# A Fourier layer stack beside its read-out head: two chunks are paired, the accumulator banks become one tile, and some read-outs are cut in half

## The chip, the cores and the metric

One core of a Trainium2 chip runs the whole program once. The metric is the device time in microseconds (us) of that run, from its first to its last instruction. The parts of the core that matter here: TensorE (PE in the profile) multiplies matrices and leaves the results in PSUM, a memory of 8 banks with 512 float32 numbers in each of 128 partitions; ScalarE (ACT) and VectorE (DVE) read PSUM, apply a function or an addition, and write to the main on-chip memory. GpSimd (POOL) and SyncE (SP) only start transfers. Each engine works through its own instructions in the program's order, and waits at an instruction until what it needs has been done by the others.

## The reference

A batch of 8 images with 8 channels of 256 x 256 is normalised, goes through a Fourier neural operator in four groups, and then through a 3 x 3 maximum:

```python
h = _gconv1x1(h, fc0_w, fc0_b)
for i in range(4):
    h1 = _spectral_conv(h, sp_w1[i], sp_w2[i])    # rfft2, mix the 12 x 12 low modes, irfft2
    h2 = _gconv1x1(h, w_w[i], w_b[i])
    h = h1 + h2
    if i < 3:
        h = _gswish(h, betas[i])
h = _gswish(_gconv1x1(h, fc1_w, fc1_b), betas[3])  # 10 -> 128 channels in each group
return _gconv1x1(h, fc2_w, fc2_b)                  # 128 -> 2 channels in each group
...
x = x + _L0_conv_ref(_gn(x), ...)
x = x + _L1_conv_ref(_gn(x))                       # 3 x 3 dilation
```

All of it is float32. The kernel has the Fourier transforms as matrix products with small tables.

## The kernel before

While the four layers of image b are computed, the "head" (fc1, Silu, fc2) of image b - 1 is computed in between, step by step. A head has 128 steps. A step is one fc1 block; at every second step there is also an fc2 block, which sums two earlier steps.

PSUM is handed out in slots of two banks, four slots in all; a small result takes a slot too and uses one bank of it:

```python
def ps_z(name):
    return ps.tile([128, 2, 512], F32, tag="z", bufs=4, name=name)

def ps_a(name):
    return ps_z(name)[:, 0, :]
```

The head. `first(n)` is an fc1 block with its two Silu read-outs by ScalarE; `second(n)` is an fc2 block with its addition by VectorE:

```python
def first(n):
    ...
    pair = [ps_z(f"p_fc1_{b}_{n}_{i}") for i in range(2)]
    for g in range(G):
        mm(pair[g // 2][:, g % 2, :], w1[part(g), blk, :], hs[k][part(g), :], start=True, stop=True)
    for i in range(2):
        nc.scalar.activation(act[:, 2 * i : 2 * i + 2, :], pair[i], AF.Silu)

def second(n):
    ...
    y, acc = box["y"], ps_a(f"p_fc2_{b}_{n}")
    for i in range(2):
        act = acts.pop(n + i)
        for g in range(G):
            mm(acc[part(g), :], w2[:, g, 15 - rb - i : 47 - rb - i], act[:, g, :], start=i == 0, stop=i == 1)
    ...                                            # y = sums + y on VectorE

for n in range(STEPS):
    ...                                            # load of a later state
    if n % 2 == 0 and n > 3:
        second(n - 4)
    first(n)
    yield
second(STEPS - 4)
second(STEPS - 2)
```

A layer goes over 11 chunks of the image, two at a time. `burst(c)` is the inverse transform along a row (L490) added to the 1x1 convolution (L487, L484 in the first layer), read out by ScalarE with Silu. `turn(c)` transposes the chunk on VectorE, `transform(k)` is the forward transform along the columns (L455) of a pair of chunks, read out half by VectorE and half by ScalarE, and `gather(k)` (L469) sums its tiles:

```python
yield "even"                                       # brings the head to an even step
for k in range((NCH + 1) // 2):
    c = 2 * k
    burst(c)
    if k > 1:
        gather(k - 2)
    yield (1,)
    turn(c)
    if c + 1 < NCH:
        burst(c + 1)
    if k > 0:
        transform(k - 1)
    yield (1,)
    if c + 1 < NCH:
        turn(c + 1)
out_["sw"] = [load_sw(l + 1, 0), load_sw(l + 1, 1)]
gather(k - 1)
transform(k)
yield 2
gather(k)
yield 1
```

`yield (1,)` asks for exactly one head step at this place; these are the exact steps. `yield 2` and the like give a weight, and head steps are spread over such places by weight; these are the loose steps. They fall between the loops over chunks, where the low modes are mixed (VectorE) and the tables of the next layer are made. The fourth layer has its own loop, one burst and two exact steps at a time. The first image has no head beside it, and the head of the last image runs alone at the end.

The engines PE, DVE and ACT keep the order in which the program is written.

Of the kernel before, what the change touches and what calls it, by code (L numbers as in the profile page):

```python
# [10 lines left out]
F32 = mybir.dt.float32  # L11
I32 = mybir.dt.int32
AF = mybir.ActivationFunctionType
ALU = mybir.AluOpType
AX = mybir.AxisListType
PSUM = bass.MemoryType.PSUM
# [18 lines left out]
NCH = 11  # L35
# [4 lines left out]
STEPS = 128  # L40
# [5 lines left out]
def fno_dilate_kernel(ctx: ExitStack, tc: tile.TileContext, a: dict, out: bass.AP):  # L46
    nc = tc.nc
# [2 lines left out]

    const = ctx.enter_context(tc.tile_pool(name="const", bufs=1))
    sb = ctx.enter_context(tc.tile_pool(name="sb", bufs=2))
    ps = ctx.enter_context(tc.tile_pool(name="ps", bufs=2, space=PSUM))
    dram = ctx.enter_context(tc.tile_pool(name="dram", bufs=2, space=bass.MemoryType.DRAM))


    def ps_z(name):
        return ps.tile([128, 2, 512], F32, tag="z", bufs=4, name=name)

    def ps_a(name):  # L60
        return ps_z(name)[:, 0, :]
# [126 lines left out]


    alone = [True]  # L190

    def copy(i, dst, src):
        if alone[0] and i % 2:
            nc.scalar.activation(dst, src, AF.Identity)  # L194
        else:
            nc.vector.tensor_copy(dst, src)  # L196
# [234 lines left out]
    def layer(b, l, out_, stored, side):  # L431
        group_in_f = l % 2 == 1

        def turn(c):

            dst = turned[:, c % 3].rearrange("p (s f x) -> p f s x", s=2, f=NQ)
            for i in range(2):
                nc.vector.transpose(  # L438
                    dst[:, 2 * i : 2 * i + 2], h[:, c, 2 * i : 2 * i + 2].rearrange("p f (s x) -> p f s x", s=2))
# [37 lines left out]
        def burst(c):  # L477
            pair = [ps_z(f"p_z_{b}_{l}_{c}_{i}") for i in range(2)]
            for f in range(NQ):
                for q in range(NQ):  # L480
                    o = pair[q // 2][part(f), q % 2, :]
                    if l == 0:
                        k = slice(32 * q, 32 * q + 6)
                        mm(o, wcn[k, :], h[k, c, f, :], start=True, stop=False)  # L484
                    else:
                        g = f if group_in_f else q
                        mm(o, wt[part(q), l, g, :], h[part(q), c, f, :], start=True, stop=False)  # L487
            for s in range(2):
                for q in range(NQ):
                    mm(pair[q // 2][:, q % 2, HW * s : HW * (s + 1)],  # L490
                       zt[part(q), 2 * c + s].rearrange("p f o -> p (f o)"), binv[part(q), :],
                       start=False, stop=s == 1)
            for i in range(2):
                dst = h[:, c, 2 * i : 2 * i + 2, :]
                if l < 3:
                    nc.scalar.activation(dst, pair[i], AF.Silu)  # L496
                else:
                    nc.scalar.activation(dst, pair[i], AF.Identity, bias=bias3)  # L498
            if l == 3:
                nc.sync.dma_start(stored[c], h[:, c].rearrange("p f w -> p (f w)"))  # L500
# [20 lines left out]
            return  # L521
        yield "even"
        for k in range((NCH + 1) // 2):
            c = 2 * k
            burst(c)
            if k > 1:
                gather(k - 2)
            yield (1,)
            turn(c)
            if c + 1 < NCH:  # L530
                burst(c + 1)
            if k > 0:
                transform(k - 1)
            yield (1,)
            if c + 1 < NCH:
                turn(c + 1)
        out_["sw"] = [load_sw(l + 1, 0), load_sw(l + 1, 1)]
        gather(k - 1)
        transform(k)
# [74 lines left out]
    def head(b, stored, stats):  # L614
        hs, acts, box = {}, {}, {}
        last = b + 1 == n_img
        if last:
            for t in (ya[:, :, 0:1], ya[:, :, HW + 1 :], ya[:, 0, :], ya[:, 17, :]):
                nc.gpsimd.memset(t, -BIG)

        def load_state(k):

            if k < NQ * NCH:
                j, c = k // NCH, k % NCH
                hs[k] = sb.tile([128, PIX], F32, tag="hs", bufs=4, name=f"hs_{b}_{k}")
                nc.sync.dma_start(hs[k], stored[c][:, PIX * j : PIX * (j + 1)])

        def first(n):

            k, blk = n // 32 * NCH + n % 32 // NBLK, n % 32 % NBLK  # L630
            act = sb.tile([128, G, 512], F32, tag="act", bufs=4, name=f"act_{b}_{n}")
            pair = [ps_z(f"p_fc1_{b}_{n}_{i}") for i in range(2)]
            for g in range(G):
                mm(pair[g // 2][:, g % 2, :], w1[part(g), blk, :], hs[k][part(g), :], start=True, stop=True)  # L634
            for i in range(2):
                nc.scalar.activation(act[:, 2 * i : 2 * i + 2, :], pair[i], AF.Silu)  # L636
            acts[n] = act

        def second(n):

            t, rb = n // 16, n % 16
            if rb == 0:
                if last:
                    y = ya[:, 1 + 2 * t : 3 + 2 * t, 1 : HW + 1]
                else:
                    y = sb.tile([128, 512], F32, tag="yp", name=f"y_{b}_{t}")
                    y = y.rearrange("p (s w) -> p s w", s=2)
                box["y"] = y
                nc.sync.dma_start(
                    y, a["x"][b].rearrange("c (p t s w) -> (c p) t s w", p=16, t=8, s=2)[:, t])  # L650
            y, acc = box["y"], ps_a(f"p_fc2_{b}_{n}")
            sums = acc.rearrange("p (s w) -> p s w", s=2)
# [3 lines that stand above are left out]
                    mm(acc[part(g), :], w2[:, g, 15 - rb - i : 47 - rb - i], act[:, g, :],  # L656
                       start=i == 0, stop=i == 1)
            if rb == 0:
                nc.vector.scalar_tensor_tensor(y, sums, b2, y, ALU.add, ALU.add)  # L659
            else:  # L660
                nc.vector.tensor_tensor(y, sums, y, ALU.add)  # L661
            if rb == 14 and last:
                for i in range(2):
                    nc.vector.bn_stats(stats[:, 2 * t + i, :], y[:, i])  # L664
                dilate_early(t)
            elif rb == 14:
                nc.vector.bn_stats(stats[:, t, :], y.rearrange("p s w -> p (s w)"))
                whole = y_rows[b % 2][:]
                nc.gpsimd.dma_start(
                    bass.AP(whole.tensor, whole.offset + (1 + 2 * t) * HW, [[16 * HW, 128], [HW, 2], [1, HW]]), y)  # L670

        load_state(0)
        load_state(1)
        for n in range(STEPS):
            if n % 32 % NBLK == 0:
                load_state(n // 32 * NCH + n % 32 // NBLK + 2)
            if n % 2 == 0 and n > 3:
                second(n - 4)
            first(n)
            yield  # L680
        second(STEPS - 4)
        second(STEPS - 2)


# [53 lines left out]
    def tail():  # L738
        if tails and next(tails[0], tails) is tails:
            tails.pop(0)  # L740
# [3 lines left out]
    with tc.manual_schedule(engines={PE, DVE, ACT}):  # L744
        d = {}
        for _ in start(0, d):
            pass
        for b in range(n_img):
            stored = [dram.tile([128, NQ * PIX], F32, tag=f"hs{c}", name=f"stored_{b}_{c}") for c in range(NCH)]
            exact, loose, ahead = 0, 0, {}  # L750
            for n in layers(b, stored, d, start(b + 1, ahead)):
                if isinstance(n, str):
                    if count[0] % 2 != (n == "odd") and step():
                        share -= 1.0
                elif isinstance(n, tuple):
                    exact += sum(n)
                    for _ in range(sum(n)):
                        if scale and step():
                            tail()
                else:  # L760
                    loose += n
                    share += n * scale if scale else 0
                    while share >= 1.0:
                        share -= 1.0
                        step()
            scale = scale or (STEPS - exact) / loose
            d = ahead
            if b + 1 < n_img:
                stats_of[b] = sb.tile([128, 8, 6], F32, tag="bn_y", name=f"bn_y{b}")
            else:  # L770
                stats_of[b] = spare[:, 16384:16480].rearrange("p (n s) -> p n s", s=6)
            heads.append((b, head(b, stored, stats_of[b])))
            alone[0] = False
        while step():
            tail()
        for t in tails:
            for _ in t:
                pass
# [151 lines left out]
```

## Time and profile before

| | |
|---|---|
| device time, median of 3 | 4005.67 us (3990.84 to 4009.22) |
| span of the profiled run | 3994.4 us, granted TensorE clock 0.978 |
| PE busy | 3717.9 us (93%) |
| ACT busy | 2813.2 us (70%) |
| DVE busy | 2566.1 us (64%) |
| DMA | 86 GB/s on average |
| fc1 blocks (L634), PE busy | 1176.2 us |
| fc2 blocks (L656), PE busy | 994.1 us |
| Silu of fc1 (L636), ACT busy | 1960.7 us in 2048 instructions, mean 1026 ns |

A row of a profile table reads: line, engine, operation, what it writes and from what, shapes, count, then the busy time and the mean of one, and then the time that the engine was idle just before, with what ended it. In a timeline a row is a run of equal instructions: its start, its length, engine, line and count, and in brackets the idle time of the engine before it. "PEld" is the load of a matrix that stays in the array; it comes ahead of a matmul and may run beside an earlier one. One float32 matmul of the program is two rows (passes) of each in the trace.

### The profile page before, as it was taken

How to read it: one execution, taken by the hardware profiler on the slowest of the kernel's cores; microseconds unless marked ns; L12 is line 12 of the kernel's file. 1: busy time of each engine (PE TensorE's matmuls, PEld its weight loads, DVE VectorE, ACT ScalarE, POOL GpSimd, SP SyncE). 2: the span in 40 equal slices, each digit the busy share in tenths (PEclk: the TensorE clock that was granted, in tenths of full speed). 3: DMA queues.
4: the chain of work that ended last, by engine and by line, in shares of the span. 5: the costliest groups of instructions: out<-in, count | busy, mean ns of one | idle time of the engine just before them, and what ended most of it. 6: DMA issues, size and time to landing. Idle time of an engine off the chain costs nothing. (4 is left out here: it accounts for less than half of the span.)

```text
span 3994.4 us, 118622 instructions
## 1 busy us (share of the span) xinstructions
PE 3717.9 (93%) x53530; PEld 1443.4 (36%) x53530; DVE 2566.1 (64%) x3679; ACT 2813.2 (70%) x2945; POOL 117.0 (3%) x202
## 2 busy tenths in 40 slices
PE   5667999999999999999999999999999999999997
PEld 2334333433333333333333333333333333333221
DVE  6775665567676666766766676666776666673533
ACT  3335777777777777776777777777777777778886
POOL 1000000000000000000000000000000000000100
PEclk8878999999999999999999999999999999999998
DMA  3014111432125222251123511244121532115311
GB/s 86 15 37 169 52 38 41 148 113 67 59 73 175 77 57 68 79 192 53 58 60 104 185 51 49 59 145 139 57 62 49 181 92 67 59 51 196 100 48 47
DMA packets 113985, 345.05 MB, mean 86 GB/s; under 512 B 15768, under 2 KB 18392, under 8 KB 98056
## 3 DMA queue, kind: packets, MB, share of 16 engines
q1 hardware_dynamic: 95288, 276.33, 22.4%
q0 software_dynamic: 18192, 61.13, 4.6%
q8 instruction: 421, 6.90, 0.7%
q14 instruction: 84, 0.69, 0.1%
HBM read 213.40 MB, written 123.74 MB: 84 GB/s over the span
## 5 line engine op out<-in xcount | busy, mean ns | idle before, releaser
L636 ACT ACTIVATE act<-p_fc 128x1024 f32<-128x1024 f32 x2048 | 1960.7, 1026 | 751.2 <-PE p_fc L634 751.2
L634 PE MATMUL p_fc<-hs,c_w 32*128 32x512 f32 x8192 | 1176.2, 631 | 11.3 <-DVE turned L196 8.5
L656 PE MATMUL p_fc<-act,c_w 128*32 128x512 f32 x8192 | 994.1, 600 | 48.1 <-ACT act L636 37.2
L634 PEld LDWEIGHTS p_fc<-hs,c_w 32*128 32x128 f32 x8192 | 386.1, 183 | 687.8 <-ACT act L636 286.5
L438 DVE STREAM_TRANSPOSE turned<-h 128x1024 f32<-128x1024 f32 x528 | 622.7, 1218 | 15.0 <-ACT h L496 14.7
L496 ACT ACTIVATE h<-p_z 128x1024 f32<-128x1024 f32 x528 | 511.9, 1021 | 123.7 <-PE p_z L490 123.1
L661 DVE TENSOR_TENSOR y<-p_fc,y 128x512 f32<-128x512 f32 x392 | 269.9, 688 | 440.8 <-PE p_fc L656 439.0
L656 PEld LDWEIGHTS p_fc<-act,c_w 128*32 128x32 f32 x8192 | 234.9, 109 | 659.7 <-issue 390.9
L490 PE MATMUL p_z<-c_binv,zt 32*128 32x256 f32 x5632 | 410.2, 404 | 0.7 <-ACT zt L194 0.6
L490 PEld LDWEIGHTS p_z<-c_binv,zt 32*128 32x128 f32 x5632 | 259.1, 186 | 305.3 <-issue 294.6
L487 PE MATMUL p_z<-h,c_wt 32*32 32x512 f32 x8448 | 358.4, 601 | 11.5 <-DVE y L661 7.8
L455 PE MATMUL p_d<-turned,c_fw 32*32 32x480 f32 (+1 forms) x9216 | 305.8, 542 | 1.4 <-DVE turned L438 1.4
L196 DVE COPY zt<-p_g 128x264 f32<-128x264 f32 x300 | 162.6, 627 | 166.1 <-PE p_g L417 90.8
L202 DVE COPY turned<-p_d 128x960 f32<-128x960 f32 x144 | 154.5, 1073 | 165.2 <-PE p_d L455 165.2
L498 ACT ACTIVATE h<-p_z,c_bias 128x1024 f32<-128x1024 f32 x176 | 186.5, 1111 | 47.8 <-PE p_z L490 47.5
L370 DVE TENSOR_REDUCE S<-turned 128x80 f32<-128x800 f32 x192 | 188.7, 983 | 4.7
L367 DVE TENSOR_TENSOR turned<-t,B 128x800 f32<-128x800 f32 x192 | 188.4, 981 | 1.2 <-DMA t<-in_spw 1.1
L331 DVE STREAM_TRANSPOSE turned<-zt 128x960 f32<-128x960 f32 x96 | 175.5, 1854 | 0.8
L455 PEld LDWEIGHTS p_d<-turned,c_fw 32*32 32x32 f32 x9216 | 121.5, 103 | 142.3 <-issue 79.2
L200 ACT ACTIVATE turned<-p_d 128x960 f32<-128x960 f32 x144 | 130.2, 904 | 57.6 <-PE p_d L455 57.6
L487 PEld LDWEIGHTS p_z<-h,c_wt 32*32 32x32 f32 x8448 | 83.9, 103 | 238.5 <-issue 62.8
L469 PE MATMUL p_u<-turned,c_stack 128*32 128x480 f32 (+1 forms) x1152 | 136.5, 545 | 15.2 <-DVE turned L202 13.1
(171 smaller groups left out, 1934.1 us busy)
## 6 DMA issues: line engine op xcount, KB each, us to landing
stored<-h SPq DMA_DIRECT2D x88, 1024.0 KB
hs<-stored SPq DMA_DIRECT2D x352, 256.0 KB
t<-in_spw SPq DMA_DIRECT2D x96, 400.0 KB
yin<-y_rows POOLq DMA_DIRECT2D x56, 512.0 KB, 5.0
h<-in_xp SPq DMA_DIRECT2D x352, 48.0 KB
turned<-in_x SPq DMA_DIRECT2D x16, 1024.0 KB
y<-in_x SPq DMA_DIRECT2D x56, 256.0 KB
y_rows<-y POOLq DMA_DIRECT2D x56, 256.0 KB, 2.3
```

Of the source, the lines that this page charges most:

```text
L367: nc.vector.tensor_tensor(pr, sw[k], bt[:, k2, k].unsqueeze(2).to_broadcast([128, G, 2 * WID, WID]), ALU.mult)
L370: nc.vector.tensor_reduce(s[k2][:, k].rearrange("p g s o -> p (g s o)"), pr.rearrange("p g m i -> p (g m) i"), AX.X, ALU.add,)
L438: nc.vector.transpose(dst[:, 2 * i : 2 * i + 2], h[:, c, 2 * i : 2 * i + 2].rearrange("p f (s x) -> p f s x", s=2))
L455: mm(pair[q // 2][part(v % 4), q % 2, : 240 * n], fw8[part(q), v, :], t[part(q), :, :, v, : NBLK * WID], start=v < 4, stop=v >= 4)
L487: mm(o, wt[part(q), l, g, :], h[part(q), c, f, :], start=True, stop=False)
L490: mm(pair[q // 2][:, q % 2, HW * s : HW * (s + 1)], zt[part(q), 2 * c + s].rearrange("p f o -> p (f o)"), binv[part(q), :], start=False, s ...
L496: nc.scalar.activation(dst, pair[i], AF.Silu)
L498: nc.scalar.activation(dst, pair[i], AF.Identity, bias=bias3)
L634: mm(pair[g // 2][:, g % 2, :], w1[part(g), blk, :], hs[k][part(g), :], start=True, stop=True)
L636: nc.scalar.activation(act[:, 2 * i : 2 * i + 2, :], pair[i], AF.Silu)
L656: mm(acc[part(g), :], w2[:, g, 15 - rb - i : 47 - rb - i], act[:, g, :], start=i == 0, stop=i == 1)
L661: nc.vector.tensor_tensor(y, sums, y, ALU.add)
```

## The change

It does four things.

1. All of PSUM is one tile of 8 banks, and the slots are cut out of it in turn. What waits for a bank is then found bank by bank, and no longer slot by slot.
2. In the first three layers, the two bursts of a pair come one after the other, then the gather, then two head steps, then the transform. The aim is that TensorE changes less often between matmul shapes.
3. The fc2 block comes at the end of each odd step and not at the start of each even one, so that two exact steps are fc1, fc1, fc2.
4. In even loose steps, the first of the two Silu read-outs is cut into its two banks, so that its first bank comes free earlier; the fc2 block that follows uses that bank.

```diff
-    ps = ctx.enter_context(tc.tile_pool(name="ps", bufs=2, space=PSUM))
+    ps = ctx.enter_context(tc.tile_pool(name="ps", bufs=1, space=PSUM))
...
+    banks = ps.tile([128, 8, 512], F32, tag="z", name="banks")
+    ring = [0]
     def ps_z(name):
-        return ps.tile([128, 2, 512], F32, tag="z", bufs=4, name=name)
+        i = ring[0]
+        ring[0] = (i + 2) % 8
+        return banks[:, i : i + 2, :]
...
+    exact_step = [False]
...
         for k in range((NCH + 1) // 2):
-            c = 2 * k
-            burst(c)
+            for c in range(2 * k, min(2 * k + 2, NCH)):
+                burst(c)
             if k > 1:
                 gather(k - 2)
+            turn(2 * k)
             yield (1,)
-            turn(c)
-            if c + 1 < NCH:
-                burst(c + 1)
+            yield (1,)
             if k > 0:
                 transform(k - 1)
-            yield (1,)
-            if c + 1 < NCH:
-                turn(c + 1)
+            if 2 * k + 1 < NCH:
+                turn(2 * k + 1)
...
-            for i in range(2):
-                nc.scalar.activation(act[:, 2 * i : 2 * i + 2, :], pair[i], AF.Silu)
+            if n % 2 == 0 and not exact_step[0]:
+                nc.scalar.activation(act[:, 0, :], pair[0][:, 0], AF.Silu)
+                nc.scalar.activation(act[:, 1, :], pair[0][:, 1], AF.Silu)
+            else:
+                nc.scalar.activation(act[:, 0:2, :], pair[0], AF.Silu)
+            nc.scalar.activation(act[:, 2:4, :], pair[1], AF.Silu)
...
-            if n % 2 == 0 and n > 3:
-                second(n - 4)
             first(n)
+            if n % 2 and n > 2:
+                second(n - 3)
             yield
-        second(STEPS - 4)
         second(STEPS - 2)
...
                     exact += sum(n)
+                    exact_step[0] = True
                     for _ in range(sum(n)):
                         if scale and step():
                             tail()
+                    exact_step[0] = False
```

## The prediction

> **What bounds the kernel now.** I read the busy times and slices of the page first, then the list of waits, then timelines of three stretches.
>
> ```profile
> PE 3717.9 (93%) x53530; PEld 1443.4 (36%) x53530; DVE 2566.1 (64%) x3679; ACT 2813.2 (70%) x2945; POOL 117.0 (3%) x202
> ...
> L636 ACT ACTIVATE act<-p_fc 128x1024 f32<-128x1024 f32 x2048 | 1960.7, 1026 | 751.2 <-PE p_fc L634 751.2
> ```
>
> TensorE sets the time: 93% busy, and ScalarE waits 751 us for it. In the list of waits its own weight loads still wait for ScalarE:
>
> ```profile
> PEld p_fc L634 <- ACT act L636: 286.5, 404, 0.8
> ...
> PEld p_fc L656 <- ACT act L636: 197.4, 230, 1.4
> ```
>
> A late weight load is not lost time while an earlier matmul still runs, so the worth of these waits has to be read from starts of blocks. First a loose stretch in which only fc1, fc1, fc2 follow each other:
>
> ```profile
> 1529.32 0.16 PEld L656 LDWEIGHTS p_fc<-act,c_w 128*32 128x32 f32 x8 [1.11 <-ACT act L636]
> ...
> 1531.18 0.31 PEld L634 LDWEIGHTS p_fc<-hs,c_w 32*128 32x128 f32 x8 [0.84 <-ACT act L636]
> ...
> 1532.41 3.77 ACT L636 ACTIVATE act<-p_fc 128x1024 f32<-128x1024 f32 x4 [0.40 <-PE p_fc L634]
> 1533.49 0.16 PEld L656 LDWEIGHTS p_fc<-act,c_w 128*32 128x32 f32 x8 [1.07 <-ACT act L636]
> ```
>
> fc2 to fc2 is 4.17 us. fc2 takes 1.86 of it (1529.32 to 1531.18); from the first fc1 to the next fc2 it is 2.31. The read-outs start 1.23 us after the first fc1 does, the first of them is done some 1.02 later, at 1533.43, and fc2 starts at 1533.49: it waits for the bank of exactly that read-out.
>
> Next one full pair of chunks in the layer loop:
>
> ```profile
> 1483.87 1.14 PE L634 MATMUL p_fc<-hs,c_w 32*128 32x512 f32 x8
> ...
> 1485.00 1.33 PE L487 MATMUL p_z<-h,c_wt 32*32 32x512 f32 x32
> ...
> 1486.26 1.15 PE L490 MATMUL p_z<-c_binv,zt 32*128 32x256 f32 x16
> ...
> 1487.33 1.01 PE L469 MATMUL p_u<-turned,c_stack 128*32 128x480 f32 x8
> ...
> 1488.16 1.90 PE L656 MATMUL p_fc<-act,c_w 128*32 128x512 f32 x16
> ...
> 1489.99 1.14 PE L634 MATMUL p_fc<-hs,c_w 32*128 32x512 f32 x8
> 1491.06 1.18 PE L487 MATMUL p_z<-h,c_wt 32*32 32x512 f32 x32
> ...
> 1492.18 1.15 PE L490 MATMUL p_z<-c_binv,zt 32*128 32x256 f32 x16
> ...
> 1493.25 2.24 PE L455 MATMUL p_d<-turned,c_fw 32*32 32x480 f32 x64
> ...
> 1495.43 1.14 PE L634 MATMUL p_fc<-hs,c_w 32*128 32x512 f32 x8
> ```
>
> One pair is 11.56 us, with hardly an idle moment. The shape behind PE changes eight times (only L469 to L656 keep theirs). Where the shape changes, an fc1 block is 1.07 us (1489.99 to 1491.06); where two fc1 follow each other without a stall, the second starts 0.88 after the first (1521.93 to 1522.81). The step between two waves of passes is 0.43, so two passes are 0.86 and a change costs about 0.21, half before and half after. The z block at 1485.00 is 0.14 longer than that at 1491.06; it waits for the transform's banks.
>
> **What the Trainium skill says.** "TensorEngine Tiling (Array Packing)", Key Properties: changing the tiling mode, not just the tile, drains the TensorEngine. The trace agrees, at about 0.21 us a change. "ScalarE: Activation LUTs", What ACT_TABLE_LOAD costs: an ACTIVATE takes 186 ns plus 0.833 ns an element, and back-to-back ones overlap by about 93. For 1024 elements that is 1.04 us; the trace has 1.026, and four in a row in 3.77, so 0.92 each. "PSUM — Partial Sum Buffer", PSUM bank collisions raise a hardware error: guard PSUM by bank and quadrant. So a slot whose first bank was read alone can be given back by halves, which is what the single tile allows; the program's list of waits shows that fc2 of a loose step then waits for the first half alone.
>
> **Part 1: the halved read-out.** From the rows above, a half is 1.03 - 0.43 = 0.60 us when it starts alone and 0.92 - 0.43 = 0.49 behind another (estimates from the trace). Then fc2's bank is free at 1.23 + 0.60 + 0.05 = 1.88 after the first fc1, and fc2 could start at 0.88 + 1.07 = 1.95, not at 2.31. That 0.36 isn't all kept. fc1 of the next pair then starts at 1.95 + 1.85 = 3.80, but its second slot is that of the third full read-out: 1.23 + 0.60 + 0.49 + 2 x 0.92 = 4.16. Followed through two pairs, with ScalarE now at 2 x 0.49 + 3 x 0.92 = 3.74 a pair: pair one is 4.15 and pair two 3.80, so 3.97 on average, 0.19 below 4.16. The built program before has 155 runs of fc1, fc1, fc2, of which 64 are in the last head alone: 155 x 0.19 = 29 us, and some 3 for pairs that get into this form. **-32 us.** There are 512 even steps, of which 29 in each of seven heads are exact, so 309 are halved; the extra instruction costs 309 x 0.07 = 22 us on ScalarE, beside TensorE.
>
> **Part 2: full pairs.** New order: z, L490, z, L490, L469, fc1, fc1, fc2, L455, and L455 to z keeps its shape. Seven changes: 11.56 less 0.21, less the 0.2 of stalls now, is 11.15 without stalls. New stalls, from z at 0: L490 starts at 0.97 and 3.11, gather at 4.19, fc1 at 5.16. Read-outs start 1.19 after L490: those of the first burst end at 3.18 and 4.10, those of the second (from 4.30) at 5.32 and 6.24. The first fc1 needs three of the four slots' history: its second half waits for 5.37 (+0.2), the second fc1 for 6.29 (hidden by that), fc2 for the full read-out that runs 6.40 to 7.42 (+0.17; exact steps are not halved). L455 starts at 9.32, the next z at 11.38. **-0.17 a pair**, for k = 2 to 4.
>
> **Part 3: the ends of the loop.** At k = 0 there is neither gather nor transform. Now it takes 1453.40 to 1461.96, 8.56 us. In the new order the second fc1's halves wait for the second burst's read-outs (5.47 and 6.39), fc2 starts at 7.36 and the next z at 9.21: **+0.65**. At k = 1, 11.27 for 11.48: **-0.2**. At k = 5 the fc1 between transform and gather is gone:
>
> ```profile
> 1514.18 2.24 PE L455 MATMUL p_d<-turned,c_fw 32*32 32x480 f32 x64
> ...
> 1516.35 0.31 PEld L634 LDWEIGHTS p_fc<-hs,c_w 32*128 32x128 f32 x8 [0.79 <-ACT act L636]
> ...
> 1517.73 0.19 PEld L469 LDWEIGHTS p_u<-turned,c_stack 128*32 128x32 f32 x8 [1.07 <-ACT turned L200]
> ...
> 1518.70 0.99 PEld L455 LDWEIGHTS p_d<-turned,c_fw 32*32 32x32 f32 x64 [0.79 <-issue]
> ```
>
> The gather needs the transform's read-outs, which end 3.5 us after its start; fc1 fills that now. Image 0, which has no head, shows the bubble bare: its transform to gather takes 3.92 us and not 2.17. Other stalls of this pair get shorter; counted through it is 11.6 for 10.59, **+1.1**. One layer: 0.65 - 0.2 - 3 x 0.17 + 1.1 = +1.05, and 3 layers x 7 images give **+22 us**.
>
> **Part 4: the entry.** In the first and third layer the loop is now entered behind fc1, fc1, and z then waits for both read-outs of the first (1576.72, with most of its passes only at 1577.64). Behind fc2 most of it falls away: 0.9 x 14 = **-12 us**. Image 0: 0.2 x 12 = **-2**. The fourth layer keeps its order on TensorE: 0.
>
> Sum: -32 + 22 - 12 - 2 = -24, so 4005.7 - 24 = **3982 us**.
>
> **The rivals.** (a) All stalls vanish: 155 x 0.36 = 56, 126 pairs x 0.21 = 26, the 12 of the entry and no bubble: about 3910. For it: PE is the bound. Against it: four slots, and two bursts that leave ScalarE four read-outs deep (3.77 us) when fc1 comes. (b) ScalarE takes over: with 76% load inside a pair, any delay of its queue meets PE several times. If each of 126 pairs had 0.5 us more stall than I count, 4045. For it: fc1, fc2 and L455 each start within 0.2 us of a read-out's end in my sums. Against it: PE's stalls overlap and don't add up. (c) It is a wash: savings in loose steps and bubbles at k = 0 and 5 cancel, 4000. My sum is between (a) and (c). That VectorE becomes the bound I hold unlikely: 48.1 us busy in the 66.7 of a layer loop (1453.40 to 1520.10, windows view).
>
> **Range and chances.** Part 1 may be 15 to 50, Part 2 and 3 together 0 to 45, the runs before spread by 18. So 3940 to 4020. Faster by over 2% is below 3926 and needs most of (a): 0.08. Slower by over 2% is above 4086: 0.03. Within: 0.89.
>
> **What would show it.** Right: fc2 to fc2 about 3.97 in loose runs; 11.4 from pair to pair; 9.2 at k = 0; some 1.4 us of PE idle ahead of the last gathers; about 309 more Silu instructions, the 512-element ones near 0.6 us; PE busy near 3700. Wrong: pairs below 11.2 or above 11.8, loose runs still at 4.16, or a longer fourth layer, which I left out.

## The result and the profile after

The kernel after takes 4052.61 us (median of 4 runs, 4044.92 to 4054.53), the kernel before 4001.77 us on the same chip. The ratio is 1.0126, 95% interval 1.0097 to 1.0154: slower by 1.3%. The prediction was 3982 us in a range of 3940 to 4020.

The lines are numbered anew in the kernel after: fc1 is L638, fc2 L665, and its y-addition L670 (L668 for the first of a sum). Of fc1's Silu read-outs, L641 and L642 are the two halves, L644 is a full first one and L645 the second. z is L493, the inverse transform L496, the column transform L461, the gather L475. The page of the kernel after, first its busy times, then its costliest Silu row:

```profile
PE 3753.9 (93%) x53530; PEld 1508.2 (37%) x53530; DVE 2557.3 (63%) x3679; ACT 2816.7 (70%) x3254; POOL 117.0 (3%) x202
...
L645 ACT ACTIVATE act<-banks 128x1024 f32<-128x1024 f32 x1024 | 1063.0, 1038 | 1.7 <-PE banks L638 1.7
```

The 309 extra read-outs are there (3254 for 2945), and the busy shares are those of before within a point. TensorE's busy time is 36 us up, where the prediction had it near 3700; nothing on the page names the loss. Two lines of the list of waits (total, times, longest):

```profile
PEld banks L638 <- ACT act L645: 176.8, 257, 0.9
...
PEld banks L665 <- ACT act L641: 106.2, 140, 0.8
```

fc1's waits for its Silu are shorter: 232 us with those for L644 (55.3), where they were 286.5. fc2's are longer: 312 us with the other three Silu lines (100.5, 62.7, 42.5), where they were 197.4. As a late load need not cost time, the starts of blocks say more. A loose stretch with fc1, fc1, fc2 alone, from the timeline of the weight loads:

```profile
1557.53 0.16 PEld L665 LDWEIGHTS banks<-act,c_w 128*32 128x32 f32 x8 [0.76 <-ACT act L642]
...
1559.38 0.31 PEld L638 LDWEIGHTS banks<-hs,c_w 32*128 32x128 f32 x8 [0.84 <-ACT act L644]
...
1561.44 0.16 PEld L665 LDWEIGHTS banks<-act,c_w 128*32 128x32 f32 x8 [0.76 <-ACT act L641]
```

fc2 to fc2 is 3.91 us here (1557.53 to 1561.44), where it was 4.17. Over all such runs of the two traces (155 before, 162 after) the mean falls from 4.24 to 4.11 us. So the halves do their work, by 0.13 us a run. One pair of the layer loop, TensorE alone:

```profile
1511.93 2.19 PE L461 MATMUL banks<-turned,c_fw 32*32 32x480 f32 x61
1513.57 0.59 PE L493 MATMUL banks<-h,c_wt 32*32 32x512 f32 x1
...
1515.16 1.15 PE L496 MATMUL banks<-c_binv,zt 32*128 32x256 f32 x16
...
1518.43 1.01 PE L475 MATMUL banks<-turned,c_stack 128*32 128x480 f32 x8
1519.37 2.29 PE L638 MATMUL banks<-hs,c_w 32*128 32x512 f32 x16
1521.68 1.92 PE L665 MATMUL banks<-act,c_w 128*32 128x512 f32 x16
1523.53 1.02 PE L461 MATMUL banks<-turned,c_fw 32*32 32x480 f32 x22
```

From L461 to L461 it is 11.60 us, before 11.56 (the last row ends with the window). And the end of the loop, where the transform of the last full pair is followed at once by its gather:

```profile
1544.55 2.24 PE L461 MATMUL banks<-turned,c_fw 32*32 32x480 f32 x64
1548.19 1.01 PE L475 MATMUL banks<-turned,c_stack 128*32 128x480 f32 x8 [1.40 <-DVE turned L208]
```

TensorE stands empty for 1.40 us ahead of L475.

To see where the time arises, the table adds up the stretches between the starts of TensorE's blocks over the seven images that have a head beside them. A loop goes from its first burst to the first block behind its last transform. The two profiled runs are 58 us apart:

| us | before | after | fc2 moved alone | pair loop alone | one tile, halves |
|---|---|---|---|---|---|
| stretches between the loops | 1326 | 1357 | 1379 | 1328 | 1316 |
| loops of layers 1 to 3 | 1437 | 1472 | 1468 | 1568 | 1445 |
| loop of the fourth layer | 548 | 543 | 534 | 550 | 556 |
| last head alone | 298 | 293 | 302 | 298 | 294 |

Between before and after, the stretches lose 31 and the loops 35; the fourth layer and the last head win 5 each. The three columns on the right are experiments told below.

### The profile page after: what moved, and what is told of

Same layout as the page of the kernel before. It is cut to its first block, busy times and chain, and to the rows that moved or that the text cites. A ratio compares the mean times of both kernels' runs of the same rounds, so it can differ in the third digit from the quotient of the medians.

```text
span 4052.7 us, 119481 instructions
## 1 busy us (share of the span) xinstructions
PE 3753.9 (93%) x53530; PEld 1508.2 (37%) x53530; DVE 2557.3 (63%) x3679; ACT 2816.7 (70%) x3254; POOL 117.0 (3%) x202
## 5 line engine op out<-in xcount | busy, mean ns | idle before, releaser
L638 PE MATMUL banks<-hs,c_w 32*128 32x512 f32 x8192 | 1252.8, 635 | 28.4 <-DVE turned L202 8.4
L645 ACT ACTIVATE act<-banks 128x1024 f32<-128x1024 f32 x1024 | 1063.0, 1038 | 1.7 <-PE banks L638 1.7
L665 PE MATMUL banks<-act,c_w 128*32 128x512 f32 x8192 | 997.7, 605 | 11.6 <-ACT h L504 9.5
L644 ACT ACTIVATE act<-banks 128x1024 f32<-128x1024 f32 x715 | 739.5, 1034 | 182.4 <-PE banks L638 162.5
L638 PEld LDWEIGHTS banks<-hs,c_w 32*128 32x128 f32 x8192 | 444.3, 184 | 647.5 <-ACT act L645 176.8
L502 ACT ACTIVATE h<-banks 128x1024 f32<-128x1024 f32 x528 | 511.7, 1021 | 222.0 <-PE banks L496 220.3
L670 DVE TENSOR_TENSOR y<-banks,y 128x512 f32<-128x512 f32 x392 | 270.2, 689 | 566.1 <-PE banks L665 318.3
L665 PEld LDWEIGHTS banks<-act,c_w 128*32 128x32 f32 x8192 | 215.5, 110 | 722.3 <-issue 343.1
L641 ACT ACTIVATE act<-banks 128x512 f32<-128x512 f32 x309 | 184.5, 597 | 345.1 <-PE banks L638 340.9
L496 PE MATMUL banks<-c_binv,zt 32*128 32x256 f32 x5632 | 408.4, 403 | 0.2 <-issue 0.2
L496 PEld LDWEIGHTS banks<-c_binv,zt 32*128 32x128 f32 x5632 | 258.2, 185 | 304.6 <-issue 295.7
L493 PE MATMUL banks<-h,c_wt 32*32 32x512 f32 x8448 | 350.3, 601 | 1.1 <-DVE y L668 0.8
L461 PE MATMUL banks<-turned,c_fw 32*32 32x480 f32 (+1 forms) x9216 | 305.5, 538 | 3.0 <-DVE turned L444 3.0
L461 PEld LDWEIGHTS banks<-turned,c_fw 32*32 32x32 f32 x9216 | 120.0, 103 | 193.3 <-issue 87.8
L642 ACT ACTIVATE act<-banks 128x512 f32<-128x512 f32 x309 | 183.1, 592 | 0.0
```

The source lines that it names most:

```text
L461: mm(pair[q // 2][part(v % 4), q % 2, : 240 * n], fw8[part(q), v, :], t[part(q), :, :, v, : NBLK * WID], start=v < 4, stop=v >= 4)
L496: mm(pair[q // 2][:, q % 2, HW * s : HW * (s + 1)], zt[part(q), 2 * c + s].rearrange("p f o -> p (f o)"), binv[part(q), :], start=False, s ...
L644: nc.scalar.activation(act[:, 0:2, :], pair[0], AF.Silu)
L645: nc.scalar.activation(act[:, 2:4, :], pair[1], AF.Silu)
```

## The experiments

**One number needed to read them.** The granted clock of TensorE differs from kernel to kernel (means from 0.969 to 0.978), and at half clock TensorE's work takes about twice as long (in b_halves the fc2 block at 3250.62 us, with 2.3 us of it at half clock, takes 3.04 us for the usual 1.92). Over 46 runs of the kernel before, the span multiplied by its own granted clock scatters by 2.3 us (standard deviation), the span itself by 5.5. I call this product the full-clock time: it shows what the order of the program costs, apart from the clock. It is worked out from the means of all runs of a kernel.

| kernel | time, us | ratio to before | mean clock | full-clock time, us |
|---|---|---|---|---|
| before | 4000 | 1 | 0.977 | 3905 |
| after | 4052.6 | 1.0126 (1.0097 to 1.0154) | 0.976 | 3952 |
| b_tile | 4014.9 | 1.0046 (1.0032 to 1.0060) | 0.976 | 3916 |
| b_halves | 4005.3 | 1.0020 (1.0010 to 1.0030) | 0.972 | 3893 |
| b_fc2end | 4068.2 | 1.0184 (1.0170 to 1.0198) | 0.977 | 3974 |
| b_pairs | 4133.4 | 1.0347 (1.0333 to 1.0361) | 0.971 | 4013 |
| a_fc2start | 4129.8 | 1.0329 (1.0313 to 1.0344) | 0.969 | 3996 |
| a_last | 4034.8 | 1.0094 (1.0079 to 1.0109) | 0.973 | 3924 |
| a_full | 4073.8 | 1.0195 (1.0173 to 1.0217) | 0.977 | 3976 |
| a_loose | 4025.4 | 1.0074 (1.0059 to 1.0089) | 0.972 | 3910 |
| a_fix | 3995.5 | 0.9987 (0.9979 to 0.9996) | 0.972 | 3881 |
| b_rows | 4006.3 | 1.0013 (1.0005 to 1.0021) | 0.978 | 3915 |
| b_fourth | 3997.7 | 0.9986 (0.9973 to 0.9999) | 0.973 | 3886 |
| a_noadd | 3995.2 | 0.9989 (0.9978 to 1.0000) | 0.976 | 3898 |
| a_loose_noadd | 3998.0 | 0.9997 (0.9989 to 1.0005) | 0.971 | 3880 |
| b_rows_late | 3987.6 | 0.9967 (0.9953 to 0.9981) | 0.978 | 3896 |
| a_fix_rows | 3976.2 | 0.9936 (0.9919 to 0.9953) | 0.978 | 3885 |

Names with b_ start from the kernel before, with a_ from the kernel after. My theory, V below, was formed from the trace of after: fc2's new place spoils the order of VectorE's work between the loops, and both ends of the loop lose time.

### The parts one by one, added to the kernel before

**b_tile**, one tile alone:

```diff
-        return ps.tile([128, 2, 512], F32, tag="z", bufs=4, name=name)
+        return banks[:, i : i + 2, :]          # ring of 8 banks in one tile
```

> The kernel before with PSUM as one tile and nothing else. Theory V (the stretches outside the loops lose their time because fc2 at the end of the odd step puts its y-addition at a later place in VectorE's queue; the loops lose theirs at both ends): within 5 us of the kernel before, about 4002, since the waits found in the trace of after are all on the readers of the very bank that is written. Rival T (one tile for all of PSUM adds waits that separate buffers don't have): 4020 to 4035, with the loss spread over the loops and the stretches alike.

Measured 4014.9: between the theories, a loss of 0.46%, of which 11 us are left at full clock (3916 for 3905). Its trace is 22 us longer than that of before: 11 of them lie in the loops of layers 1 to 3 and the rest is spread. So the tile isn't free, as I had thought, but it isn't the main loss either. What the tile's cost consists of was not followed up.

**b_halves**, the halved read-outs on top of it:

```diff
+            if n % 2 == 0 and not exact_step[0]:
+                nc.scalar.activation(act[:, 0, :], pair[0][:, 0], AF.Silu)
+                nc.scalar.activation(act[:, 1, :], pair[0][:, 1], AF.Silu)
+            else:
+                nc.scalar.activation(act[:, 0:2, :], pair[0], AF.Silu)
```

> The kernel before with one tile and the even step's first read-out halved outside the loops. Theory V: 3980 to 4003, because halving frees a bank some 0.45 us earlier and harms nothing by itself. Rival H (309 more Silu instructions at about 0.2 us of fixed cost each lengthen ScalarE's queue, and that is the loss outside the loops): 4025 to 4035, all of it outside the loops.

Measured 4005.3, 10 us less than with the tile alone and 23 less at full clock (3893 for 3916). The stretches between the loops fall by 10 against before. Rival H is out; theory V's range is missed by 2 us. The halves gain, and more than half of it goes to a lower clock, 0.972 for 0.976.

**b_fc2end**, fc2 at the end of the odd step, four separate slots as before:

```diff
-            if n % 2 == 0 and n > 3:
-                second(n - 4)
             first(n)
+            if n % 2 and n > 2:
+                second(n - 3)
```

> The kernel before with fc2 at the end of the odd step instead of the start of the even one, nothing else. Theory V: the stretches outside the loops get about 30 us longer (as in the kernel after), so 4025 to 4040, with TensorE idle ahead of the matmuls of the mixing, and VectorE idle ahead of its y-additions longer than before. Rivals T and H: no loss from this part, 3995 to 4005.

Measured 4068.2: 72 us lost, more than theory V said. By the table, 53 lie between the loops and 31 in them; the fourth layer wins 14. This part alone is slower than the whole change. The fc2 block itself has moved ahead in the program's order: it now stands before whatever the layer has between two steps, and no longer behind it. The y-additions show it; first before, then this kernel, each from the list of VectorE's waits (total, times, longest):

```profile
DVE y L661 <- PE p_fc L656: 439.0, 310, 6.5
```

```profile
DVE y L661 <- PE p_fc L656: 663.9, 352, 5.7
```

VectorE stands 225 us longer ahead of the same additions, with whatever is queued behind them. (Ahead of the first addition of each sum, L659, it stands 24 us less.) In the stretches between the loops alone, its idle time ahead of all y-additions is 271 us, before 150.

**b_pairs**, the pair loop alone (the loop as in the diff of the change):

```diff
-            burst(c)
+            for c in range(2 * k, min(2 * k + 2, NCH)):
+                burst(c)
...
+            yield (1,)
             yield (1,)
             if k > 0:
                 transform(k - 1)
```

> The kernel before with the loop in pairs (two bursts, turn, two head steps, transform), nothing else. Theory V: the loops lose what they lose in the kernel after, some 35 us from the first and the last turn of the loop (about 30 from the empty TensorE ahead of the last gathers), the stretches outside nothing: 4030 to 4045. Rivals T and H: the same loss in the loops, so this run tells only whether the losses of the parts add up; if it is near 4002, the loss at the ends of the loop needs fc2's new place as well.

Measured 4133.4. The stretches lose nothing, as theory V said, but the loops lose 131 us and not 35. Some 26 of these are half clock in the first layer's loops. By the starts of the blocks a pair takes 12.41 us (second layer of image 3), and the transform starts 2.15 us after the second fc1, where 1.07 is free of waits. The second fc1 stops halfway:

```profile
1546.24 0.30 PEld L632 LDWEIGHTS p_fc<-hs,c_w 32*128 32x128 f32 x4 [0.89 <-DVE y L659]
```

Its second slot is the one that fc2, two blocks ahead of it, took, and the y-addition that reads that fc2 (1545.53 to 1546.18) stands on VectorE behind two transposes. In the kernel after, fc2 comes behind the two fc1, and they don't need its slot. The losses of the parts don't add up; each of the two orders mends part of what the other breaks.

### One part undone in the kernel after

**a_fc2start**, fc2 back at the start of the even step everywhere:

```diff
+            if n % 2 == 0 and n > 3:
+                second(n - 4)
             first(n)
-            if n % 2 and n > 2:
-                second(n - 3)
```

> The kernel after with fc2 back at the start of the even step: the pair loop, the one tile and the halved read-outs stay. Theory V: outside the loops it returns to the kernel before with halves (about 40 us less than after over the seven images), inside the loops it costs what the pair loop alone cost (+137 on before), so 4125 to 4145. Rival (the losses of the pair loop came from its being tried with full read-outs and four buffers, and one tile mends them): 4015 to 4060.

Measured 4129.8: the pair loop needs fc2 at the end of the step, with or without the tile. The stretches fall to 1315 us, level with b_halves.

**a_last**, for the last single chunk one head step on each side of the transform:

```diff
             yield (1,)
-            yield (1,)
+            if 2 * k + 1 < NCH:
+                yield (1,)
             if k > 0:
                 transform(k - 1)
             if 2 * k + 1 < NCH:
                 turn(2 * k + 1)
+            else:
+                yield (1,)
```

> The kernel after with one head step moved, for the last, single chunk alone: one step ahead of the column transform of chunks 8 and 9 and one after it, instead of both ahead. Theory V: TensorE no longer stands empty for some 1.4 us between that transform and its gather, 21 times, so 4015 to 4030. Rival (the wait only moves: the transform now waits for the turn of chunk 9, or the last transform for the turn of chunk 10): 4045 to 4055, with a new gap of the same size ahead of a transform.

Measured 4034.8: 18 us less than after, and 29 less at full clock (3924 for 3952). The empty 1.40 us is gone, 21 times; no new gap of this size takes its place, and the loops fall by 26. The clock took the difference (0.973 for 0.976).

**a_full**, full read-outs, one tile kept:

```diff
-            if n % 2 == 0 and not exact_step[0]:
-                ...
+            nc.scalar.activation(act[:, 0:2, :], pair[0], AF.Silu)
```

> The kernel after with full read-outs everywhere, one tile kept. Theory V: the halves earned some 15 to 25 us outside the loops even here, so 4065 to 4080. Rival H (the halves lengthen ScalarE's queue): 4020 to 4035.

Measured 4073.8: the halves are worth 21 us in the kernel after too, 23 at full clock, as on before.

**a_loose**, fc2 at the end of the step only in exact steps:

```diff
+            if n % 2 == 0 and box.get("n", 0) <= n - 4:
+                second(box.get("n", 0)); box["n"] = box.get("n", 0) + 2
             first(n)
-            if n % 2 and n > 2:
-                second(n - 3)
+            if n % 2 and n > 2 and exact_step[0] and box.get("n", 0) <= n - 3:
+                second(box.get("n", 0)); box["n"] = box.get("n", 0) + 2
```

> The kernel after with fc2 at the end of the odd step only inside the loops and the fourth layer; outside them it is at the start of the even step, as before. One tile, halves and pair loop stay. Theory V: the stretches outside the loops fall to those of before with halves, some 40 us less than in after, and the loops keep 483 and 487 us: 4008 to 4022. Rival (the stretches are longer for another reason, the place of the last gathers or the phase in which the loop leaves ScalarE's queue): 4045 to 4060.

Measured 4025.4, 27 us less than after; at full clock 42 less (3910 for 3952), which is the figure that theory V gave for the stretches. The rival is out: it is fc2's place. In the trace the stretches fall by 78 us and the loops of layers 1 to 3 grow by 52. The edit also moves one fc2 block from the stretches into each loop, 21 blocks of 1.85 us or 39 us; without these the stretches fall by 39, and what is left of the loops' growth is about what they lose to half clock.

Most of the 42 us shows ahead of two matmuls of a stretch that wait for VectorE's work, the spectrum (L346) and the mixing (L392). Their rows of the profile table, of after and then of a_loose:

```profile
L346 PE MATMUL banks<-turned,c_eh_f 128*32 128x120 f32 x2304 | 92.7, 306 | 41.6 <-DVE turned L337 41.6
L392 PE MATMUL banks<-F,c_fold 32*32 32x120 f32 x1024 | 36.7, 285 | 84.4 <-DVE F L384 78.1 <-ACT act L642 6.0
```

```profile
L346 PE MATMUL banks<-turned,c_eh_f 128*32 128x120 f32 x2304 | 93.3, 308 | 32.2 <-DVE turned L337 32.2
L392 PE MATMUL banks<-F,c_fold 32*32 32x120 f32 x1024 | 36.7, 285 | 65.3 <-DVE F L384 63.1 <-ACT act L642 1.4
```

TensorE is idle 28 us less ahead of these two. One stretch (image 3, between the second and third layer) in detail. In the kernel after, VectorE and then the spectrum:

```profile
1554.48 0.69 DVE L670 TENSOR_TENSOR y<-banks,y 128x512 f32<-128x512 f32 x1 [3.25 <-PE banks L665]
...
1555.82 0.39 DVE L478 COPY zt<-banks 128x240 f32<-128x240 f32 x1
1556.25 1.86 DVE L337 STREAM_TRANSPOSE turned<-zt 128x960 f32<-128x960 f32 x1
1559.58 0.75 DVE L668 SCALAR_TENSOR_TENSOR y<-banks,c_b,y 128x512 f32<-128x512 f32 x1 [1.47 <-PE banks L665]
...
1566.35 3.69 PE L346 MATMUL banks<-turned,c_eh_f 128*32 128x120 f32 x96 [1.71 <-DVE turned L337]
```

In a_loose:

```profile
1541.29 0.41 DVE L478 COPY zt<-banks 128x240 f32<-128x240 f32 x1 [1.94 <-PE banks L475]
1541.74 1.95 DVE L337 STREAM_TRANSPOSE turned<-zt 128x960 f32<-128x960 f32 x1
1543.95 0.69 DVE L670 TENSOR_TENSOR y<-banks,y 128x512 f32<-128x512 f32 x1 [0.26 <-PE banks L665]
...
1552.80 3.38 PEld L346 LDWEIGHTS banks<-turned,c_eh_f 128*32 128x32 f32 x96 [0.76 <-ACT act L645]
```

The spectrum (L346) needs four transposes (L337), and these need the copy of the last gather (L478). In after, fc2 and its addition are queued ahead of that gather: VectorE waits 3.25 us, adds, and only then copies; before the next transposes it waits another 1.47 us for the next fc2. In a_loose the copy comes first, and the additions wait 0.26 us and, for the next one at 1547.80, 0.63. From the last transform (1549.13 and 1537.24) to L346 it is 17.2 us against 15.6, with the same blocks of the head in between. The copy starts 2.64 us later in after. Only 0.90 of that is the addition and what follows it on VectorE. The other 1.74 arise on TensorE, where fc2 stands ahead of the gather as well: L475 starts 5.05 us behind the last transform, in a_loose 3.31. So fc2's place acts in the order of two engines.

### What fc2's place acts through

**a_late**, the y-addition queued one step later:

```diff
             first(n)
+            if "add" in box:
+                box.pop("add")()
             if n % 2 and n > 2:
-                second(n - 3)
+                box["add"] = second(n - 3)     # returns its addition
```

> The kernel after with one thing moved: the y-addition that reads an fc2 is queued on VectorE one head step later, behind the work of the stretch that lies between, so that VectorE no longer stands before it until fc2 is done. All TensorE work, the loops, the halves stay in their order. Theory V (VectorE takes its work in order, and the y-addition holds up the transposes and the mixing behind it): outside the loops 20 to 40 us of the loss go, 4010 to 4035. Rival R (fc2 at that place holds TensorE itself, because its last Silu has only just been queued): no change outside the loops, 4045 to 4060.

Measured 4324.3, but it says nothing about the question. With one ring of slots, a loop's bursts write the bank of fc2 again before the queued addition reads it, so the addition takes other sums, and the waits are no longer those of the kernel after. The edit needed more banks than there are.

**a_noadd** and **a_loose_noadd**, both leaving out y-additions between the loops (245 and 224 additions, since fc2 falls a little differently to loops and stretches; the sums in y are then incomplete):

```diff
-            if rb == 0:
+            if not exact_step[0] and not last:
+                pass
+            elif rb == 0:
```

> The kernel after, leaving out the y-additions that belong to head steps outside the loops (some 36 in each of seven images, 0.65 us of VectorE each); all else stays. Both theories: faster than after (4053), since VectorE has less to do. To be read beside a_loose_noadd. Theory V: equal to it within 12 us, apart from the granted clock, because fc2's place acts through the y-addition alone. Rival R (fc2 at the end of the step holds TensorE until the second Silu is done): still 25 to 45 us slower than a_loose_noadd.

> The kernel with fc2 at the start of the even step outside the loops (4025), leaving out the same y-additions. Theory V: 3960 to 4010, by less than a_noadd falls below after, so that the two meet. Rival R: it falls by as much as a_noadd, and 25 to 45 us stay between them.

Measured 3995.2 and 3998.0: level. At full clock 3898 and 3880, so 18 us are left of the 42 that fc2's place costs with the additions there. Neither expectation holds in full. The y-addition carries 25 of the 42 us, and the idle time of TensorE agrees: ahead of L346 and L392 it is 22.3 and 62.4 us in a_noadd, 22.3 and 62.3 in a_loose_noadd, so the 28 us between after and a_loose are gone. The other 18 must be something that acts without the addition. Two things fit: fc2's own block ahead of urgent work on TensorE, as in the stretch above, and TensorE's longer wait for the Silu ahead of fc2 (the four lines of L665 behind Silu add up to 321 us in a_noadd and 271 in a_loose_noadd). Neither was tested, and it stays open.

### Putting it together

**a_fix**: a_loose, a_last, and the first two chunks one by one:

```diff
+            if k == 0:
+                for c in (0, 1):
+                    burst(c)
+                    yield (1,)
+                    turn(c)
+                continue
```

> The kernel after with three parts undone together: fc2 at the start of the even step outside the loops, one head step between the last column transform of a pair and its gather, and the first two chunks one by one as before. The pair loop stays for chunks 2 to 9. Theory V, by adding the single results (27 and 18 us less than after, and some 15 to 17 us for the first two chunks): 3988 to 4000, level with the kernel before. Rival (the three lie on the same wait, or what they save goes into half clock of TensorE): 4005 to 4020.

Measured 3995.5, as added up. At full clock the first two alone would give 3952 - 42 - 29 = 3881, and 3881 is measured: undoing the pair order at k = 0 brings nothing. The loop of the second layer says the same: 489 us in a_loose, less the 9 that a_last brought there, is the 480 measured. From the first burst to the third, k = 0 of that layer takes 10.32 us in a_fix and 10.36 in a_loose, both with the one fc2 block more. The longer k = 0 belongs to fc2's place: in b_fc2end, which has no pair order, it is 9.44 us, against 9.36 in after and 8.57 before.

**b_fourth**: b_halves with fc2 at the end of the step in the fourth layer alone (the condition of a_loose, with a flag set in that loop).

> The kernel before with one tile and halves (4005 us), and fc2 at the end of the odd step in the fourth layer's loop alone. Theory V (at that place fc2 costs only where VectorE's work is on the path, and in the fourth layer it is not): the fourth layer falls from 556 to about 540 us over seven images, 3988 to 3996. Rival (the fourth layer's gain needs the other stretches in the new order): 4002 to 4010.

Measured 3997.7. The fourth layer falls from 556 to 544, by a little less than expected. There the place at the end of the odd step pays, also without the rest of the new order. That nothing of VectorE is on the path there is theory V's reason; it was not tested by itself.

**b_rows** and **b_rows_late** look for the lost clock. In the first layer the burst's matmuls have 6 live rows of 32:

```diff
-                        k = slice(32 * q, 32 * q + 6)
+                        k = part(q)                                             # b_rows, and h set to 0
+                        k = part(q) if b else slice(32 * q, 32 * q + 6)         # b_rows_late
```

> The kernel before with one tile and halves (4005 us measured, mean granted clock 0.972), and the matmuls of the first layer's bursts take all 32 rows of each tile instead of 6; the rows added have zero weights, so the result and the number and shape of the instructions on TensorE stay, and h is cleared once at the start. Theory C (the half clock of TensorE comes when the monitor sees little activity, and 6 of 32 rows is little): the granted clock goes to 0.977 or more and the time to 3983 to 3992. Rival P (the half clock answers to dense work, as a power limit would): the clock stays at 0.972 or falls, and the time is 4003 to 4010.

> The kernel before with one tile and halves (4005, clock 0.972), with all 32 rows in the first layer's bursts from the second image on; the first image keeps 6 rows, so h need not be cleared. Theory C (little activity brings the half clock): clock 0.976 to 0.978, 3983 to 3992. Rival P: clock 0.972, 4003 to 4010.

b_rows has its clock back (0.978) but not its time (4006.3), because setting h to 0 delays the first image by 18 us (89.2 us to the first burst, 70.7 in b_halves). b_rows_late has both: 3987.6, 18 us less than b_halves. Windows at a first-layer loop, first of b_halves and then of b_rows_late (length, then busy times of PE, PEld, DVE, ACT, POOL, then the granted clock, and the share and GB/s of DMA):

```profile
3246.00:3256.00 10.00, 10.00 (x116) 2.79 (x112) 2.21 (x4) 6.85 (x9) 0.00 (x0) 0.83 0.23 73
```

```profile
3236.00:3246.00 10.00, 10.00 (x132) 3.51 (x128) 3.25 (x4) 8.29 (x11) 0.00 (x0) 1.00 0.18 61
```

**a_fix_rows**, the same on a_fix:

> The kernel after with the three parts undone (3996, clock 0.972) and all 32 rows in the first layer's bursts from the second image on. Theory C: clock 0.976 to 0.978, 3972 to 3983, faster than the kernel before by 0.5 to 0.7 per cent. Rival P: 3993 to 4000.

Measured 3976.2, 0.64% faster than before, and the fastest kernel of this study; what it keeps of the change is the tile, the halves, the pair loop for chunks 2 to 9, and fc2's new place in exact steps. Part of the gain is the 32 rows, which are no part of the change; what they would give the kernel before alone was not run.

## Why the prediction was wrong

- **The step that failed is a missing term: the sum has none for fc2's new place outside the loops.** Part 1 prices the loose stretches by halves alone, "-32 us". The text says what each stretch gains when TensorE waits less for a Silu, and takes for granted that the new place is neutral. It costs 53 us between the loops by itself (b_fc2end), and 42 at full clock in the kernel after (a_loose), of which the y-additions carry 25. From the forecast of -24 to the +51 measured it is 75 us; as an estimate from the single runs, 42 of them are this term, 13 the loops, 11 the tile and 9 the halves (tile and loops may overlap). None of the three signs of being wrong that the text lists came up: the loss was at a place that it didn't watch.
- **The sentence behind it:** "That VectorE becomes the bound I hold unlikely: 48.1 us busy in the 66.7 of a layer loop". The window was taken in the loop and used for the stretches. A window on a stretch would not have shown it either: VectorE is busy 36.24 of 53.00 us (1400 to 1453). It is on the path while it stands and waits ahead of an addition, with the copy and the transposes queued behind. The timeline of what ends last in a stretch shows this, and I had not followed it.
- **Part 1's own mechanism was right.** fc2 starts earlier behind its half, by 0.13 us in the mean over all runs of fc1, fc1, fc2 where the text has 0.19, and the halves bring 23 us at full clock, on before and on after alike, where the text has 32. The tile that they need costs 11 of these, which the text doesn't count.
- **Part 2, "-0.17 a pair", is +0.04.** The part from gather to transform came out as counted (5.10 us from L475 to L461, counted as 5.13). What failed is "L455 to z keeps its shape": transform and z take 1.64 + 1.59 = 3.23 us without a shape change between them, where the text counts 2.06 + 0.97 = 3.03; apart, each between changes and without a stall, they took 2.17 + 1.12 = 3.29. Image 0 of the kernel before has no head between the two and shows the same 1.64 + 1.59 (185.29, 186.93, 188.52), so this could have been read beforehand. The text's two sums don't agree either: "11.15 without stalls" and its stalls of 0.2 and 0.17 make 11.52, not 11.38.
- **Part 3** has the right sign, and the bubble of "some 1.4 us" is there at 1.40, with its worth shown by a_last. In the second layer k = 0 takes 0.79 us longer (predicted 0.65), k = 1 is 0.48 shorter (0.2), the three pairs add 0.12, and the stretch from the last burst to the end of the loop 1.77 (1.1): 2.2 a loop, where the text has 1.05. The cause given for k = 0, the new order of the bursts, isn't borne out by a_fix; fc2's place is enough. All loops together lose 35 us, not 22.
- **Part 4** came out at the place itself: at the entry of the third layer the z block behind fc2 is shorter (1.42 for 1.98 us in image 3), and the second fc1 ahead gives way after 0.97 us instead of 1.35. That is 0.94 us where the text has 0.9, and about as much in the first layer. It is hidden in the sums by what the stretches and k = 0 lose.
- **The fourth layer**, set to 0, wins 5, and 14 where fc2 alone is moved.
- **The rivals:** (b) came nearest in time, 4045, at another place: it had 0.5 us more stall in each pair, and pairs are only 0.04 longer. That fc2 waits longer for its Silu outside the loops may be its share of the truth, within the 18 us left open above. (a) and (c) took the stretches between the loops for gains too.
- **The clock** was not in the sum. Between before and after it is some 5 us of the 51 only, but it hid 13 of the 23 us of the halves and 11 of a_last's 29.

## What to carry to other kernels

When an operation moves, ask on every engine that works behind it what now stands ahead of what: an engine that is 68% busy can set the end while it waits in order for a result that nobody needs yet. Put the addition that may wait behind the copy that others wait for, and the matmul that may wait behind the one that opens the chain. Try parts both together and apart: at full clock the pair loop cost 108 us without fc2's move and gained about 8 beside it (3976 in a_full, where b_tile and fc2's move add up to 3984).

## What the runs showed of the hardware

The granted clock falls to one half in pieces of 3.4 us, or multiples, and can do so while TensorE has work without a gap: in the window of b_halves above it is busy for 10.00 of 10.00 us. "TensorE: Matmul & The Clock Gate" of the Trainium skill, Part 1: The HAM clock gate, says that the array's clock is gated to half after an idle window of about 3.4 us, and that activity brings it back. The length agrees with this trace; the idleness doesn't. With the matmuls of 6 rows made 32 rows (same count, same shape of output, zeros added), the trace of b_rows_late has no half clock in the first layer's loops of the seven images that follow image 0, against 20.5 us in that of b_halves, and the mean clock goes from 0.972 to 0.978. On a_fix it goes from 34.1 us to 6.8, not to none. So what counts here as activity depends on the rows in use, not only on whether matmuls run.

It also means that a gain on TensorE need not arrive: fewer waits came with a lower clock in b_halves, a_last, a_loose and a_fix. Behind image 0, the half clock of these four traces falls into the loops of the first and fourth layer and into the last head, but for one piece of 3.4 us; the loops of the second and third layer have none. Why it comes outside the first layer isn't settled.

Last, two blocks in the same tiling shape did not follow each other for free. The transform and z, both 32x32, take 3.23 us one behind the other and 3.29 with other shapes between, so only 0.06 of an estimated 0.21 us a change is gained, in the kernel after and in image 0 of before alike. "TensorEngine Tiling (Array Packing)", Key Properties, speaks of a drain when the mode changes; that a block of other weights in the same mode can cost nearly as much is what these traces add. It was not tested by itself, and z's first weight loads also carry waits there.
